# Graph attention on one core: rows of long neighbour lists searched whole, a slot index built in four parts, and a fourth slot for one row tile

## The chip, the cores and the metric

The kernel runs on one core of a Trainium2 chip. The metric is the device time of one launch in microseconds (us), taken as the median of several runs. Profiles come from one execution each; their times are us from the start of the span.

## The reference: what is computed

A pre-norm attention layer over a sparse graph. There are 16 batches of 1024 nodes with 512 features, and one adjacency matrix for all of them, in which a node has few neighbours (and always itself).

```python
h = relu(layernorm(x))                             # x: (16, 1024, 512)
q, k, v = h @ Wq + bq, h @ Wk + bk, h @ Wv + bv    # Wq, Wk, Wv: (512, 512); 8 heads of 64
scores = einsum('bihd,bjhd->bhij', q, k) / 8
scores = scores + where(adj == 0, -1e9, 0)         # adj: (1024, 1024), 0 or 1, diagonal 1
out = x + einsum('bhij,bjhd->bihd', softmax(scores), v)
```

## The kernel before

The kernel doesn't form the 1024 x 1024 scores. It sorts the nodes by degree and cuts them into eight tiles of 128 rows. Tile 0 holds the nodes with most neighbours, tile 7 those with fewest. Every row of tile t gets `CAPS[t]` slots, one neighbour each. Keys and values of a batch lie in DRAM as rows of 1024 numbers; a slot is one gather of 128 such rows. Tile 0 has rows with more neighbours than slots; what is left over is cut into pieces of four, which are worked on as one more tile, number -1.

The slots of a tile are worked on in units of two to four. A unit is (tile, first slot, slots); unit 0 is tile 7 and unit 2 is tile 5.

```python
CAPS = (11, 8, 6, 5, 4, 3, 3, 2)
PIECE = 4
PIECES = 17
LIST = CAPS[0] - 1 + PIECE * PIECES
ROUNDS = -(-LIST // 8)                             # 10
UNITS = (
    (7, 0, 2), (6, 0, 3), (5, 0, 3), (4, 0, 4), (3, 0, 3), (3, 3, 2), (2, 0, 3), (2, 3, 3),
    (1, 0, 4), (1, 4, 4), (0, 0, 4), (-1, 0, 4), (0, 4, 4), (0, 8, 3),
)
LAST_ORDER = (10, 11, 12, 13, 8, 9, 6, 7, 4, 5, 3, 2, 1, 0)   # the order of units in the last batch
POOL_FOLDS = (2, 3, 8, 9, 10, 11, 12)              # units whose folds of one slot are GpSimd's
BY_VECTOR = {2: 1, 3: 0, 4: 1}                     # slots of a unit that VectorE weighs; ScalarE the others
BY_VECTOR_LAST = {2: 1, 3: 1, 4: 2}                # the same in the last batch
```

What is done for a unit, with the line under which the profile lists it:

```python
def gather(i, s):         # L866, GpSimd's queue; a row's own node comes by SyncE's queue (L864)
    nc.gpsimd.indirect_dma_start(out=G[i][:, s]..., in_=KV[b % len(KV)][:], in_offset=on(ap=index[:, c + s : c + s + 1], axis=0))
def multiply(i):          # L876, DVE: keys times the tile's queries, which lie in PSUM
    nc.vector.tensor_tensor(k, k, Q[b, t][:, None, :].to_broadcast([P, count, D]), ALU.mult)
def score(i):             # L880, DVE: sums over each head
    nc.vector.tensor_reduce(weights[:, w, :], heads(G[i][:, :count, 0, :]), AX.X, ALU.add)
def exponent(i):          # L884, ACT
    nc.scalar.activation(weights[:, w, :], weights[:, w, :], AF.Exp, scale=HD**-0.5)
def weigh_v(i):           # L896, DVE: values of some slots times their weights
def weigh_s(i, s):        # L902, ACT: one slot, eight instructions
def fold(i, first, n):    # L907, DVE or GpSimd: adds n slots to n others
    engine = nc.gpsimd if n == 1 and i % NU in POOL_FOLDS else nc.vector
    engine.tensor_tensor(v[:, 0:n], v[:, 0:n], v[:, first : first + n], ALU.add)
# folds of a unit: {2: ((1, 1),), 3: ((2, 1), (1, 1)), 4: ((2, 2), (1, 1))}[count]
```

Per tile of rows and batch there are, besides: `load_x` (L590, GpSimd's queue), `stats` (L599, DVE), `variance` (L608, DVE), `power` (L611, GpSimd), `shift` (L615, DVE), `norm` (L625, ACT), `flip` (L632, PE transposes), `unflip` (L637, ACT), the projections to keys, values and queries (L642, PE), `evict_kv` (L653, ACT), `store_kv` (L665), `residual` (L966, GpSimd) and `put_out` (L969, GpSimd's queue). Keys and values of a batch are made while the batch before is attended to; PSUM holds the queries of two tiles.

The preparation, done once, ranks the nodes by degree, and tells each sorted row its node and the layernorm's numbers (table `told`), its own index and its first eight neighbours (table `lists`). Both tables are scattered through DRAM. For tile 0 all neighbours are needed, in falling order of a number that stands for the node:

```python
def spots():                                   # the slots of tiles 1 to 7
    merge("lists")
    for t in range(1, NT):
        c = first_col[t, 0]
        nc.vector.tensor_copy(spot[:, c : c + CAPS[t]], after["lists"][:, t, : CAPS[t]])
    slots(1)                                   # their index, in one piece
def long_rows():                               # L726: the 128 longest rows of adj, gathered
    ...
blocks, most = 16, 16
def long_blocks(k):
    row = LONG[0][:, 0, :]
    if k == 0:                                 # L734
        nc.vector.scalar_tensor_tensor(row, row, 0.0, key_row, op0=ALU.not_equal, op1=ALU.mult)
        return
    for c in range(4 * k - 4, 4 * k):          # L739 to L741: sixteen largest of each block of 64
        block = row.rearrange("p (k c) -> p c k", c=blocks)[:, c, :]
        got = LONG[0][:, 1, most * c : most * (c + 1)]
        nc.vector.max(got[:, 0:8], block)
        nc.vector.match_replace(block, got[:, 0:8], block, 0.0)
        nc.vector.max(got[:, 8:16], block)
def longest(k):                                # L747 to L751: rounds 1 to 9, eight numbers each
    row = LONG[0][:, 1, : most * blocks]       # 256 columns
    if k == 1:                                 # the first eight are known from the lists: take them out
        nc.vector.tensor_copy(found0[:, 0:8], after["lists"][:, 0, near])
        nc.vector.scalar_tensor_tensor(row, row, found0[:, 7:8], row, op0=ALU.is_lt, op1=ALU.mult)
    nc.vector.max(found0[:, ts(k, 8)], row)
    if k < ROUNDS - 1:
        nc.vector.match_replace(row, found0[:, ts(k, 8)], row, 0.0)
```

After the rounds, `count_pieces`, `owners`, `copy_owners` and `pieces` (DVE) with three small PE steps (L775, L785, L792) make the list of pieces, and `slots(0)` the index of tiles 0 and -1.

The order of the instructions on each engine isn't that of the text. A small list scheduler in the kernel sorts all steps by a place given to each, with rough lengths, and checks that a buffer is free; every engine then runs its instructions in that order.

## Time and profile before

| | |
|---|---|
| device time, median of three runs | 1755.13 us (1753.89 to 1758.23) |
| profiled span | 1752.1 us, 19712 instructions |
| mean granted TensorE clock | 0.97 |
| DMA | 531.73 MB, mean 303 GB/s |
| GpSimd gathers of slots (L866) | 608, 1030 ns each |
| ACT weighing (L902) | 4768 instructions, 340 ns each |

A line of the profile names the source line, the engine, the operation, the output and the inputs, the shape and the count. In the order of time, the first number is the start, the second the length, and square brackets at the end hold the idle time of the engine before the instruction and what ended it. GpSimd is called POOL, VectorE DVE, ScalarE ACT, TensorE PE. A busy time counts an instruction from start to end, also while it is held up inside.

### The profile page before, as it was taken

The page shows a single profiled execution, that of the slowest core. Times are in us where ns is not written, and L with a number is a line of the kernel's source. Part 1 is how long each engine was busy: PE and PEld are TensorE (multiplying, and loading weights), DVE is VectorE, ACT ScalarE, POOL GpSimd, SP SyncE. Part 2 cuts the span into 40 slices and gives each one's busy share as a digit, 9 for nine tenths or more (in the row PEclk, how much of TensorE's full clock was granted, in tenths as well). Part 3 has the DMA queues.
Part 4 walks back from the last instruction along what each step waited for, and adds up shares of the span by engine and source line. Part 5 has one row for each costly group of instructions (what it writes and reads, how often), then busy time and mean ns, then how long its engine had stood idle before and what let it go on. Part 6 is the DMA issues. An engine that isn't in the chain of part 4 may idle for free.

```text
span 1752.1 us, 19712 instructions
## 1 busy us (share of the span) xinstructions
PE 1618.9 (92%) x4295; PEld 751.8 (43%) x4295; DVE 1558.5 (89%) x1922; ACT 1489.1 (85%) x5556; POOL 1330.9 (76%) x1235
## 2 busy tenths in 40 slices
PE   6979898999999999999999999999999999999796
PEld 3444444444444444444444444444444444444333
DVE  5788989899898979989898998989989898988897
ACT  5359989898898988889898888989899898889965
POOL 4757778787787868877787877878787787877774
PEclk9989999999999999999999999999999999999989
DMA  5388889888898988988898888989988898888894
GB/s 219 132 321 293 309 292 344 309 324 316 287 329 304 339 298 309 323 284 327 305 350 303 304 304 293 346 318 328 322 294 313 293 346 304 318 311 290 310 359 169
DMA packets 150742, 531.73 MB, mean 303 GB/s; under 512 B 19916, under 2 KB 19916, under 8 KB 150616
## 3 DMA queue, kind: packets, MB, share of 16 engines
q0 software_dynamic: 109840, 390.70, 62.5%
q1 hardware_dynamic: 40776, 139.71, 21.7%
q8 instruction: 36, 0.59, 0.1%
q14 instruction: 90, 0.74, 0.1%
HBM read 429.51 MB, written 100.82 MB: 303 GB/s over the span
## 4 chain that ended last, share of the span: by engine, by line
PE 45%; DVE 18%; POOL 8%; ACT 6%; issue 4%; DMA 3%; POOLq 0%; DVEq 0%
PE pq L642 15%; PE pk L642 12%; PE pv L642 8%; DVE g L876 5%; ACT g L902 4%; PE acc L925 4%; DVE g L907 3%; DVE weights L880 3%; PE pht L632 3%; POOL g L866 3%; DVE shift L615 3%; DMA out_dram<-x,perm 2%; POOL x L966 2%; POOL g L907 1%; DVE g L896 1%
## 5 line engine op out<-in xcount | busy, mean ns | idle before, releaser
L902 ACT ACTIVATE g<-g,weights 128x64 f32<-128x64 f32 x4768 | 1180.3, 340 | 3.2 <-DVE weights L889 2.2
L866 POOL DMA_INDIRECT g<-kv,index x608 | 626.1, 1030 | 204.6 <-issue 143.5
L876 DVE TENSOR_TENSOR g<-g,pq 128x1536 f32<-128x1536 f32 (+2 forms) x208 | 389.1, 1872 | 95.4 <-PE pq L642 90.9
L642 PE MATMUL pq<-wq,hT 128*128 128x512 f32 x1024 | 460.3, 592 | 0.0
L642 PE MATMUL pk<-wk,hT 128*128 128x512 f32 x960 | 439.0, 601 | 1.8 <-ACT hT L637 1.7
L642 PE MATMUL pv<-wv,hT 128*128 128x512 f32 x960 | 431.6, 592 | 0.0
L880 DVE TENSOR_REDUCE weights<-g 128x32 f32<-128x2048 f32 (+2 forms) x224 | 423.2, 1890 | 0.6
L907 DVE TENSOR_TENSOR g<-g 128x512 f32<-128x512 f32 (+1 forms) x271 | 281.1, 1038 | 21.9 <-ACT g L902 19.8
L642 PEld LDWEIGHTS pq<-wq,hT 128*128 128x128 f32 x1024 | 194.7, 190 | 228.0 <-issue 224.7
L642 PEld LDWEIGHTS pk<-wk,hT 128*128 128x128 f32 x960 | 185.8, 194 | 212.9 <-issue 206.0
L642 PEld LDWEIGHTS pv<-wv,hT 128*128 128x128 f32 x960 | 182.5, 190 | 205.3 <-issue 201.9
L969 POOL DMA_INDIRECT out_dram<-x,perm x128 | 148.1, 1157 | 79.2 <-DMA out_dram<-x,perm 34.2
L625 ACT ACTIVATE h<-x,shift,rstd 128x512 f32<-128x512 f32 x120 | 91.3, 809 | 91.5 <-DVE shift L615 91.5
L590 POOL DMA_INDIRECT x<-in_x_dram,perm x128 | 135.9, 1062 | 34.9 <-issue 32.4
L907 POOL TENSOR_TENSOR g<-g 128x512 f32<-128x512 f32 x120 | 153.5, 1279 | 10.7 <-DVE g L907 7.2
L632 PE MATMUL pht<-ident,h 128*128 128x128 f32 x512 | 86.2, 308 | 80.2 <-ACT h L625 78.2
L632 PEld LDWEIGHTS pht<-ident,h 128*128 128x128 f32 x512 | 68.3, 158 | 139.5 <-ACT h L625 104.5
L896 DVE TENSOR_TENSOR g<-g,weights 128x512 f32<-128x512 f32 (+1 forms) x134 | 114.5, 855 | 2.2 <-ACT weights L884 1.7
L653 ACT COPY kvt<-pv 128x512 f32<-128x512 f32 x120 | 69.2, 577 | 43.0 <-PE pv L642 43.0
L966 POOL TENSOR_TENSOR x<-x,o 128x512 f32<-128x512 f32 x67 | 86.3, 1288 | 25.0 <-DVE o L957 22.1
L925 PE MATMUL acc<-g,ident 128*128 128x512 f32 x170 | 95.6, 682 | 2.8 <-POOL g L907 2.8
L637 ACT COPY hT<-pht 128x512 f32<-128x512 f32 x128 | 72.1, 575 | 26.9 <-PE pht L632 26.9
(231 smaller groups left out, 1187.0 us busy)
## 6 DMA issues: line engine op xcount, KB each, us to landing
g<-kv SPq DMA_DIRECT2D x128, 512.0 KB
kv<-kvt SPq DMA_DIRECT2D x120, 512.0 KB
g<-kv,index POOLq DMA_INDIRECT x608, 7.2
adj<-in_adj_dram SPq DMA_DIRECT2D x8, 512.0 KB
x_first<-in_x_dram SPq DMA_DIRECT2D x8, 256.0 KB
x<-in_x_dram,perm POOLq DMA_INDIRECT x128, 4.6
out_dram<-x,perm POOLq DMA_INDIRECT x128, 5.0
wk<-in_L_gnn_Wk_dram SPq DMA_DIRECT2D x1, 1024.0 KB
```

The lines of the kernel that those rows point to most:

```text
L590: nc.gpsimd.indirect_dma_start(out=X[n][:], out_offset=None, in_=x_rows, in_offset=on(ap=perm[:, t : t + 1], axis=0), element_offset=b * N * D
L632: nc.tensor.transpose(PH[n][:, c, :], hn[:, ts(c, P)], ident)
L642: nc.tensor.matmul(pt, HT[n][:, c, :], W[name][:, c, :], start=False, stop=(c == DC - 1))
L866: nc.gpsimd.indirect_dma_start(out=G[i][:, s].rearrange("p j d -> p (j d)"), out_offset=None, in_=KV[b % len(KV)][:], in_offset=on(ap=inde ...
L876: nc.vector.tensor_tensor(k, k, Q[b, t][:, None, :].to_broadcast([P, count, D]), ALU.mult)
L880: nc.vector.tensor_reduce(weights[:, w, :], heads(G[i][:, :count, 0, :]), AX.X, ALU.add)
L896: nc.vector.tensor_tensor(v, v, own.to_broadcast([P, n, H, HD]), ALU.mult)
L902: nc.scalar.activation(v[:, h, :], v[:, h, :], AF.Identity, scale=weights[:, c + s, h : h + 1])
L907: engine.tensor_tensor(v[:, 0:n], v[:, 0:n], v[:, first : first + n], ALU.add)
L925: nc.tensor.matmul(ACC[b, home], owner_t if t < 0 else ident, v[:, s, :], start=(u == parts_of(home)[0] and s == 0), stop=(u == parts_of(h ...
L966: (nc.vector if shares_in(b, B, t) and b == B - 1 else nc.gpsimd).tensor_tensor(rows, rows, add, ALU.add)
L969: nc.gpsimd.indirect_dma_start(out=out_rows, out_offset=on(ap=perm[:, t : t + 1], axis=0), in_=X.pop(b * NT + NT - 1 - t)[:], in_offset=No ...
```

## The change

Four things are different. Tile 5 has four slots in place of three, so unit 2 has four. The long rows are searched whole: the cut into blocks is gone, and each of the nine rounds reads the full row of 1024 columns; the first eight, which the lists hold already, are taken out beforehand as before. The slot index is made in four parts, each as soon as what it needs is there, so that gathers of the short tiles can start before the long rows are done. And the places in the plan are others: the `told` table is scattered before the `lists`, the x of batch 0 is loaded later, and most places of the repeated steps moved a little.

```diff
-CAPS = (11, 8, 6, 5, 4, 3, 3, 2)
+CAPS = (11, 8, 6, 5, 4, 4, 3, 2)
...
-    (5, 0, 3),
+    (5, 0, 4),
...
+PARTS = ((7, 6, 5), (4, 3), (2, 1), (0, -1))
...
-        add(("tell", t), "POOL", 1.3, -35.76 + 0.3 * t, ...
-        add(("spread", t), "POOL", 1.3, -28.64 + t, ...
+        add(("tell", t), "POOL", 1.3, -70.00 + 0.3 * t, ...
+        add(("spread", t), "POOL", 1.3, -30.76 + t, ...
...
-    for k in range(1, 5):
-        add(("long_blocks", k), "DVE", 2.0, -32.13 + 0.1 * k, [("long_blocks", k - 1)], [("g", -2)])
     for k in range(1, ROUNDS):
-        known = [("long_blocks", 4), ("spots",)] if k == 1 else [("longest", k - 1)]
-        add(("longest", k), "DVE", 1.1 if k == 1 else 0.8, --0.41 + 0.5 * k, known, [("g", -2)])
+        known = [("longest", 0), ("spots", 0)] if k == 1 else [("longest", k - 1)]
+        add(("longest", k), "DVE", 4.0 if k == 1 else 2.5, -3.25 + 0.5 * k, known, [("g", -2)])
...
-        p = (b - 1) * NU + j * rate if b > 0 else j * rate - 19.58 if b == 0 else 1.5 * j - 44.63
+        p = (b - 1) * NU + j * rate if b > 0 else j * rate - 8.00 if b == 0 else 1.5 * j - 44.25
...
-        stored = [("spots",) if t > 0 else ("slots", 0)] + [("store_kv", (b or -1) * NT + j) for j in range(NT)]
+        stored = [next(("spots" if t > 0 else "slots", k) for k, p in enumerate(PARTS) if t in p)] + [("store_kv", (b or -1) * NT + j) for j in range(NT)]
...
-        def spots():
-            merge("lists")
-            for t in range(1, NT):
+        def spots(k):
+            if k == 0:
+                merge("lists")
+            for t in PARTS[k]:
...
-            slots(1)
+            slots(k)
...
-        def longest(k):
-            row = LONG[0][:, 1, : most * blocks]
+        def longest(k):
+            row = LONG[0][:, 0, :]
+            if k == 0:
+                nc.vector.scalar_tensor_tensor(row, row, 0.0, key_row, op0=ALU.not_equal, op1=ALU.mult)
+                return
```

What the new places make of the order, as far as the prediction speaks of it (x8 and x9 are the first and second tile of the next batch; u2 is unit 2 of the batch at hand):

| engine | before | after |
|---|---|---|
| DVE, preparation | list_of 7, search in blocks, spots, longest 1 to 8, stats 8, longest 9, stats 9, count_pieces, variance 4, owners, shift 4, ..., multiply 0 | list_of 7, others, longest 0, spots 0, spots 1, longest 1, spots 2, longest 2, stats 8, ..., longest 6, shift 4, ..., longest 8, multiply 0, ..., longest 9, shift 5, ... count_pieces, multiply 4, ..., owners, ..., pieces, slots 3 |
| PE, preparation | ..., flip 5, 6, 7, three steps of the pieces, flip 8, 9, keys of 8 | ..., flip 8, 5, 9, 6, keys of 8, queries of tile 5, flip 10, ... |
| ACT, preparation | copy_row key, unflip of the third tile, rank_of 4 to 7 | copy_row key, norm, rank_of 4 to 7, unflip of the third tile |
| DVE, each batch | weigh_v u3, multiply u4, ..., multiply u5, fold u3, score u5, shift | weigh_v u2, ..., weigh_v u3, fold u2 (1024), multiply u4, ..., multiply u5, fold u3, shift, score u5 |
| PE, each batch | queries of tiles 7 and 6, add_up, queries of tile 5 | queries of tiles 7 and 6, keys of x8, add_up, queries of tile 5 |
| ACT, each batch | ..., weigh_s u2 0, evict x9, ... | ..., evict x9, weigh_s u2 0, weigh_s u2 1, evict x9, exponent u3, weigh_s u2 2 |
| POOL, each batch | fold u2, ..., fold u2, ..., power, fold u3, residual | put_out, fold u2, power, residual, ..., fold u3 |

## The prediction

> **What bounds the kernel now.** I read the page first, then the busy times in one window per batch, then the chain that ended last, then DVE, PE, ACT and POOL in order of time through one batch, then the preparation before 110 us.
>
> The page's first part shows four engines loaded, none full:
>
> ```profile
> PE 1618.9 (92%) x4295; PEld 751.8 (43%) x4295; DVE 1558.5 (89%) x1922; ACT 1489.1 (85%) x5556; POOL 1330.9 (76%) x1235
> ```
>
> The windows (window, length, then busy us and count of PE, PEld, DVE, ACT, POOL, granted clock, DMA share, GB/s):
>
> ```profile
> 98.00:202.00 104.00, 92.59 (x252) 44.43 (x253) 92.31 (x142) 84.24 (x308) 74.67 (x71) 0.93 0.87 312
> 409.00:512.00 103.00, 97.04 (x260) 45.11 (x259) 93.13 (x108) 91.92 (x350) 81.14 (x74) 0.98 0.88 315
> 1650.00:1752.00 102.00, 76.69 (x174) 32.77 (x174) 87.09 (x90) 68.07 (x280) 64.48 (x59) 0.88 0.70 263
> ```
>
> A batch repeats every 103.2 us (the first multiply of unit 4 stands at 445.36 in one batch and 548.58 in the next). PE has 97 us of work in it and DVE 93. A batch is longer than either, so a loop through several engines sets it. The chain of waits shows which: it runs on PE from 459 to 494, on DVE from 494 to 508, over ACT's layernorm to PE at 509, on PE to 434, and over DVE and POOL back to PE at 458. DVE in order of time (start, duration, line, shape, idle before and its releaser):
>
> ```profile
> 420.01 1.75 DVE L876 TENSOR_TENSOR g<-g,pq 128x1536 f32<-128x1536 f32 x1 [1.17 <-PE pq L642]
> 432.97 0.21 DVE L947 TENSOR_REDUCE sums<-weights 128x8 f32<-128x32 f32 x1 [1.25 <-ACT weights L884]
> 433.98 2.29 DVE L876 TENSOR_TENSOR g<-g,pq 128x2048 f32<-128x2048 f32 x1 [0.56 <-PE pq L642]
> 445.36 1.75 DVE L876 TENSOR_TENSOR g<-g,pq 128x1536 f32<-128x1536 f32 x1 [4.13 <-PE pq L642]
> 454.93 2.44 DVE L615 SCALAR_TENSOR_TENSOR shift<-mv,rstd 128x2 f32<-128x2 f32 x1 [0.54 <-POOL rstd L611]
> ```
>
> At units 0 to 3 DVE waits for PE's query projections, 4.13 us before unit 4. From unit 4 on it is the engine that makes PE wait. I therefore cut the batch at unit 4's multiply and at the end of the shift that releases the last layernorm, and asked for DVE's busy time in both parts:
>
> ```profile
> 445.36:507.95 62.59, 60.55 (x60) 1.00 0.88 319
> 507.95:548.50 40.55, 33.33 (x48) 0.96 0.89 319
> ```
>
> Full stretch: DVE busy 60.6 of 62.6. Slack stretch: 33.3 of 40.6, 7.2 idle, with PE full (39.65 busy of 40.55). The loop is DVE 62.6 plus PE 40.6. The 60.6 is not all work, as the next two pairs show:
>
> ```profile
> 456.10 1.25 POOL L966 TENSOR_TENSOR x<-x,g 128x512 f32<-128x512 f32 x1
> ...
> 464.45 1.27 POOL L966 TENSOR_TENSOR x<-x,g 128x512 f32<-128x512 f32 x1
> ```
>
> ```profile
> 463.88 2.40 DVE L907 TENSOR_TENSOR g<-g 128x512 f32<-128x512 f32 x1
> ```
>
> A shift of two columns is 0.15 us when alone (422.29) and was 2.44; a fold of 512 is 0.68 and was 2.40. Both end as POOL's additions end (457.35, 465.72). In this stretch such stretched records add 1.4, 2.3, 1.7, 0.5, 1.1 and 1.1, about 8 us.
>
> **What the Trainium skill says.** "SBUF — State Buffer", section "Who interferes with whom": a DVE instruction with two SBUF inputs contends with a GpSimd instruction that reads SBUF, and whoever comes second blocks for the whole instruction. The trace agrees with the two pairs above; multiplies, whose second input is in PSUM, keep 2.29 us beside POOL folds (493.95). "VectorE: DVE Perf Modes", section "The perf-mode tier table (the rule you actually need)": fp32 tensor_tensor and tensor_reduce run at one element per cycle, 2293 ns for 2048. The trace has 2.28 and 2.27, so a slot costs its elements and nothing hides in a faster mode. "Perfetto Trace Analysis", section "Optimization Strategy", says to look for gaps within a regime, since the most contended engine may change over time; that is the cut above.
>
> **The change, part by part.**
>
> *The fourth slot of tile 5 (unit 2), each batch.* DVE: multiply and score go from 1536 to 2048 elements (1.75 to 2.28 and 1.73 to 2.27, +1.07). Units of four give one slot to DVE's weighing (+0.69) and one fold of 1024 to DVE (+1.21): +3.0 us. ACT still weighs three slots. POOL loses one of two folds (-1.28) and issues one more gather (0.95 + 0.30): nothing. DMA moves 0.52 MB more per batch of some 32 MB, +1.6%. PE is unchanged. All 3.0 us lie between the last shift and unit 4's multiply, in the stretch with 7.2 us idle. By the built order, the DVE work from unit 4's multiply to that shift is the same set of instructions in both kernels, and so is PE's set from there to unit 4's queries. So I expect the slot not to lengthen the loop.
>
> Does it fit? In the new order the queries of unit 2 come one projection later (428.1 in the old clock instead of 424.5), those of unit 3 and 4 stay at 434 and 445.2. DVE from 434: multiply 2.2, two folds and the small ones 1.8, score 2.2, weighings 1.2, fold 1.15, so about 443. But ACT evicts the keys of the next batch's second tile, from PE at 438.1, ahead of unit 2's weighings: 0.5 + three weighings at 1.93 + one eviction 0.5 + an exponent 0.2 ends at 445.1, the fold at 446.4. Unit 4 starts about 1 us late.
>
> *The full stretch.* POOL's second fold of unit 2, beside which a DVE fold of 1024 took 2.58 instead of 1.22 (450.68), is gone: -1.3. The layernorm's power stands earlier in POOL's order, ahead of a residual and folds, and the shift on DVE right behind unit 3's fold. So the flip that made PE wait 2.0 us at 458.27 comes in time, and DVE starts unit 6 at about 456.3, as its queries arrive, not at 458.19: -1.9, part of it the same time as the -1.3. Against +1 for the fold, the loop loses about 1 us. The other stretched records may fall better or worse. I take -1.0 per batch with an uncertainty of 1.3, over the 14 to 15 batches from the first unit 4 on: -14 us, give or take 19.
>
> *The preparation.* DVE's search of the long rows, in order of time before:
>
> ```profile
> 73.84 1.22 DVE L734 SCALAR_TENSOR_TENSOR adj_long<-adj_long,rows 128x1024 f32<-128x1024 f32 x1 [5.39 <-DMA adj_long<-in_adj_dram,perm]
> 75.10 0.27 DVE L739 MAX8 adj_long<-adj_long 128x8 f32<-128x64 f32 x1
> ...
> 92.62 0.48 DVE L748 SCALAR_TENSOR_TENSOR adj_long<-adj_long,found 128x256 f32<-128x256 f32 x1
> ...
> 104.97 0.15 DVE L615 SCALAR_TENSOR_TENSOR shift<-mv,rstd 128x2 f32<-128x2 f32 x1
> ```
>
> The blocks go: 75.1 to 88.5, -13.4 us. The rounds now read 1024 columns instead of 256. A MAX8 of 1024 has 1228 ns (list_of's row) against 424, a MATCH_REPLACE8 I estimate at 408 + 800. So a round is about 2.6 instead of 0.98 us, eight rounds +12.8, the masking and the last maximum +1.5. The search costs as much as before. The index in four parts adds two pairs of small instructions, +0.7.
>
> What moves is order. The first part of the index needs only the lists, and stands at about 77 instead of 92. But the first multiply follows eight rounds on DVE, and comes at about 106, as before (106.87). What gains is PE. The shift for batch 1's first layernorm, before the last thing to end (104.97), now follows six rounds. PE stood idle before it:
>
> ```profile
> 103.37 0.59 PE L775 MATMUL p_before<-has,owner_t 128*128 128x1 f32 x2 [7.77 <-DVE owner_t L772]
> ```
>
> Counting DVE on from lists at 75, with 2.6 a round and 0.9 a statistic, that shift ends at 99.5. From its flip to unit 4's queries PE has 28.6 us of work, one wait of about 1, so these end at 130 instead of 134.9: -5. Against it: the longest-row pieces and part of the slots (some 4 us of DVE) now fall into batch 0's full stretch, which had 5 us idle; ACT ranks tiles before it copies the third flipped tile, so PE stores batch 0's keys some 6 us later, and the lists start 3 us later, which the tables scattered first only partly win back. Net -2, between -6 and +4. Loading batch 0's x later costs nothing, its first use is behind those stores.
>
> *The tail.* Unit 2 stands in the last four of the last batch, where DVE and PE alternate without slack: +1.07 +0.6 on DVE: +1.7.
>
> Sum: 1755.1 - 14 - 2 + 1.7 = 1741; a little caution gives 1742.
>
> **Rivals.** First, DVE is the bound and every microsecond of the slot counts: 15 x 3.0 + 1.7, no gain at the loop: about 1800. For it: DVE at 93 of 103 and continuous from 463 to 512. Against it: the 7.2 us idle exactly where the slot falls. Second, the ACT order in front of unit 2's weighings takes the slack: +1 to +2 per batch without the gains behind it, about 1770 to 1780. For it: 92 of 103 busy, DVE waits 1.25 us for it at 432.97 already. Third, PE becomes the bound at 97.6 us per batch, its waits all gone: 15 x -5.6, about 1672. Against it: the 4 us wait at 508.85 behind DVE remains. Fourth, only preparation counts and the loop stays: 1755.
>
> **Range and chances.** The loop's uncertainty of 19 and the preparation's 4 give 1716 to 1774. Faster by over 2% (below 1720) needs -2.3 us per batch: 0.15. Slower by over 2% (above 1790) is the first rival: 0.05. Within: 0.80.
>
> **What would show it.** Right: unit 4's multiply repeating every 101 to 103 us, DVE's idle at units 0 to 3 down to 4 or less, the flip at 458 without a wait, PE's hole before 104 gone and batch 0's unit 4 at 129 to 132. Wrong: the period above 104, DVE or PE waiting for ACT's weighing of unit 2, or more stretched folds and shifts than about 8 us a batch.

## The result: half a per cent slower, and where the time lies

The changed kernel takes 1764.97 us (median of 4 runs, 1762.67 to 1765.71), the kernel before 1754.51 (1753.84 to 1758.23): ratio 1.0053, 95% interval 1.0036 to 1.0070. I had forecast 12.5 us less; it is 10.5 us more. The range held it, the sign was wrong. Two further comparisons of the same two kernels gave 1.0059 (1.0039 to 1.0078) and 1.0058 (1.0045 to 1.0071).

"Batch n" below runs from unit 4's multiply of batch n to that of the next. Two pairs of traces (that of the first comparison, whose chips are not on record, and e5 and e6 of the experiments, both from one chip) place the loss:

| us | before | after | before, second pair | after, second pair |
|---|---|---|---|---|
| unit 4 of batch 0 starts | 134.9 | 136.4 | 135.3 | 137.4 |
| batch 0 | 102.8 | 103.9 | 102.8 | 103.9 |
| batch 3 | 103.2 | 111.9 | 104.3 | 109.5 |
| batch 12 | 103.6 | 107.1 | 102.7 | 107.0 |
| the other eleven of batches 1 to 13, mean | 103.97 | 103.67 | 103.53 | 103.50 |
| from unit 4 of batch 14 to the end | 164.0 | 164.3 | 165.2 | 164.4 |
| span | 1752.1 | 1763.9 | 1749.0 | 1760.7 |

The eleven ordinary batches gained 3.3 us in all in one pair and 0.3 in the other. Batches 3 and 12 lost 12.2 and 9.6, the preparation with batch 0 2.6 and 3.2.

### The profile page after: what moved, and what is told of

The parts are those of the page before. It is cut to its first block, busy times and chain, and to the rows that moved or that the text cites. A ratio compares the mean times of both kernels' runs of the same rounds, so it can differ in the third digit from the quotient of the medians.

```text
span 1763.9 us, 19726 instructions
## 1 busy us (share of the span) xinstructions
PE 1629.2 (92%) x4297; PEld 752.7 (43%) x4297; DVE 1574.6 (89%) x1892; ACT 1495.9 (85%) x5556; POOL 1305.7 (74%) x1236
## 4 chain that ended last, share of the span: by engine, by line
PE 34%; DVE 15%; DMA 11%; POOL 10%; issue 8%; ACT 8%; POOLq 0%; DVEq 0%; ACTq 0%
PE pq L642 12%; PE pk L642 8%; DMA g<-kv,index 7%; ACT g L890 6%; PE pv L642 6%; DVE g L895 5%; PE acc L913 4%; POOL g L854 4%; DVE weights L868 4%; DVE g L864 3%; DMA out_dram<-x,perm 3%; POOL x L954 3%; PE pht L632 2%; DMA x<-in_x_dram,perm 2%; POOL out_dram L957 1%
## 5 line engine op out<-in xcount | busy, mean ns | idle before, releaser
L854 POOL DMA_INDIRECT g<-kv,index x624 | 643.3, 1031 | 202.1 <-issue 141.5
L868 DVE TENSOR_REDUCE weights<-g 128x32 f32<-128x2048 f32 (+2 forms) x224 | 432.5, 1931 | 0.6
L864 DVE TENSOR_TENSOR g<-g,pq 128x2048 f32<-128x2048 f32 (+2 forms) x208 | 396.4, 1911 | 33.4 <-PE pq L642 15.7
L895 DVE TENSOR_TENSOR g<-g 128x512 f32<-128x512 f32 (+1 forms) x286 | 305.4, 1068 | 20.0 <-ACT g L890 19.6
L957 POOL DMA_INDIRECT out_dram<-x,perm x128 | 133.1, 1040 | 86.0 <-DMA out_dram<-x,perm 29.9
L590 POOL DMA_INDIRECT x<-in_x_dram,perm x128 | 129.6, 1013 | 46.8 <-issue 34.4
L632 PE MATMUL pht<-ident,h 128*128 128x128 f32 x512 | 89.9, 310 | 79.2 <-ACT h L625 75.3
L895 POOL TENSOR_TENSOR g<-g 128x512 f32<-128x512 f32 x105 | 134.7, 1283 | 18.4 <-DVE g L895 16.7
L653 ACT COPY kvt<-pk 128x512 f32<-128x512 f32 x120 | 69.1, 576 | 47.4 <-PE pk L642 46.9
```

Of the source, the lines that this page charges most:

```text
L590: nc.gpsimd.indirect_dma_start(out=X[n][:], out_offset=None, in_=x_rows, in_offset=on(ap=perm[:, t : t + 1], axis=0), element_offset=b * N * D
L632: nc.tensor.transpose(PH[n][:, c, :], hn[:, ts(c, P)], ident)
L854: nc.gpsimd.indirect_dma_start(out=G[i][:, s].rearrange("p j d -> p (j d)"), out_offset=None, in_=KV[b % len(KV)][:], in_offset=on(ap=inde ...
L957: nc.gpsimd.indirect_dma_start(out=out_rows, out_offset=on(ap=perm[:, t : t + 1], axis=0), in_=X.pop(b * NT + NT - 1 - t)[:], in_offset=No ...
```

## The profile after

The first part of the page of the changed kernel, busy times of the five engines:

```profile
PE 1629.2 (92%) x4297; PEld 752.7 (43%) x4297; DVE 1574.6 (89%) x1892; ACT 1495.9 (85%) x5556; POOL 1305.7 (74%) x1236
```

DVE is up 16.1 us, where the slots alone are 45 (15 x 3.0); shorter stretched records (1.3 us a batch, below) make up some 20 of the difference. POOL is down 25.2.

The windows of the changed kernel (window, length, then busy us and count of PE, PEld, DVE, ACT, POOL, granted clock, DMA share, GB/s): batch 9, cut where the prediction cut its batch, and batch 3.

```profile
1077.61:1138.90 61.29, 57.24 (x151) 25.59 (x149) 59.53 (x61) 57.27 (x217) 47.13 (x45) 1.00 0.87 317
1138.90:1181.93 43.03, 42.08 (x110) 20.17 (x111) 36.08 (x50) 35.98 (x137) 31.67 (x30) 0.92 0.89 318
445.44:557.29 111.85, 102.80 (x263) 47.69 (x262) 92.55 (x110) 94.47 (x358) 84.39 (x77) 0.94 0.84 301
```

The same two stretches of batch 9 in the kernel before:

```profile
1070.19:1132.04 61.85, 57.52 (x153) 26.06 (x151) 59.82 (x60) 56.94 (x215) 51.45 (x46) 1.00 0.89 318
1132.04:1172.95 40.91, 40.01 (x108) 19.33 (x109) 33.34 (x50) 35.82 (x137) 29.94 (x28) 0.96 0.88 315
```

In this batch the full stretch is 0.6 shorter and the slack stretch 2.1 longer. In the slack stretch DVE has 2.7 us more work, the slot, and still 7 us idle: the slot fits, as forecast. But PE is busy 2.1 us longer, with two more records, at a granted clock of 0.92 instead of 0.96.

What DVE waited for between 300 and 1600 us (releaser, us in all, times, longest), before:

```profile
DVE g L876 <- PE pq L642: 80.4, 45, 4.1
DVE sums L947 <- ACT weights L884: 16.2, 13, 1.2
DVE shift L615 <- POOL rstd L611: 4.8, 9, 0.5
DVE st L599 <- DMA x<-in_x_dram,perm: 0.3, 1, 0.3
```

and after:

```profile
DVE sums L935 <- ACT weights L872: 29.2, 13, 2.4
DVE st L599 <- DMA x<-in_x_dram,perm: 23.2, 13, 2.7
DVE o L945 <- PE acc L913: 14.2, 11, 2.3
DVE g L864 <- PE pq L642: 12.5, 13, 3.1
DVE shift L615 <- POOL rstd L611: 12.0, 7, 4.2
DVE g L864 <- DMA g<-kv,index: 7.7, 10, 3.0
```

The idle at the queries of units 0 to 4 is mostly filled. Five waits are new or grown: the row sum in front of unit 4 waits 2.2 us a batch for an exponent, the statistic behind unit 4's multiply waits 1.8 for a load of x, the output of a tile waits for PE's sums, the shift for GpSimd's power, and multiplies wait for gathers. DVE around unit 4 after, in order of time:

```profile
1178.88 0.22 DVE L935 TENSOR_REDUCE sums<-weights 128x8 f32<-128x40 f32 x1 [2.41 <-ACT weights L872]
...
1180.79 1.23 DVE L895 TENSOR_TENSOR g<-g 128x1024 f32<-128x1024 f32 x1 [0.50 <-ACT g L890]
1181.93 1.75 DVE L864 TENSOR_TENSOR g<-g,pq 128x1536 f32<-128x1536 f32 x1
```

Unit 4's queries were done at 1180.94 (here and below: when PE starts its next record), so the multiply is 1.0 late; before, it followed its queries by 0.2 in every batch. ACT in the same time shows why:

```profile
1173.84 0.59 ACT L653 COPY kvt<-pk 128x512 f32<-128x512 f32 x1 [2.94 <-PE pk L642]
1174.33 3.93 ACT L890 ACTIVATE g<-g,weights 128x64 f32<-128x64 f32 x16
1178.16 0.56 ACT L653 COPY kvt<-pv 128x512 f32<-128x512 f32 x1
1178.63 0.23 ACT L872 ACTIVATE weights<-weights 128x32 f32<-128x32 f32 x1
```

ACT stands 2.94 us before the keys of the next batch's second tile, and the weighings and the exponent come behind them.

PE at its second wait of batch 9, before:

```profile
1132.94 1.97 PE L632 MATMUL pht<-ident,h 128*128 128x128 f32 x8 [3.96 <-ACT h L625]
1134.70 1.77 PE L925 MATMUL acc<-g,ident 128*128 128x512 f32 x2
...
1136.67 3.60 PE L642 MATMUL pk<-wk,hT 128*128 128x512 f32 x8
```

and after:

```profile
1139.85 1.12 PE L632 MATMUL pht<-ident,h 128*128 128x128 f32 x4 [4.81 <-ACT h L625]
1140.76 1.92 PE L913 MATMUL acc<-g,ident 128*128 128x512 f32 x2
1142.47 1.06 PE L632 MATMUL pht<-ident,h 128*128 128x128 f32 x4
...
1143.99 4.47 PE L642 MATMUL pq<-wq,hT 128*128 128x512 f32 x8
```

Behind the wait PE is slow in both kernels: eight transposes take 1.97 or 2.18 us (1.04 at 96.77 us in e6), two sums 1.77 or 1.92 (1.02 at 1151.91 before), and in this batch after also the first projection, 4.47 for 3.60. That last differs from batch to batch: of batches 4 to 11 two have such a slow projection before (4.54 and 4.55) and two after (4.44 and 4.47). The next 32.6 us of PE are the same to 0.01 in both kernels (1140.10 to 1172.75, and 1148.30 to 1180.94). "TensorE: Matmul & The Clock Gate", section "HAM oscillation — how this bites in real kernels", says that an idle gap of PE of more than about 3.4 us throttles it, so that the work behind the gap starts at half clock. The trace agrees: behind waits of 3.96 and 4.81 the transposes and sums take nearly twice as long, and the granted clock is below 1 in this stretch and 1.00 in the other.

Over batches 4 to 11 the means are, by stretches:

| us | before | after | before, second pair | after, second pair |
|---|---|---|---|---|
| unit 4 to the end of PE's second wait | 63.56 | 62.49 | 62.98 | 62.35 |
| DVE in it: stretched records, excess | 8.18 | 6.75 | 7.96 | 6.73 |
| DVE in it: waits | 1.68 | 2.52 | 1.40 | 2.45 |
| PE's first wait in it | 1.69 | 0.53 | 1.49 | 0.75 |
| from there to the end of the first projection (slow start) | 7.49 | 7.57 | 7.59 | 7.61 |
| from there to the end of unit 4's queries | 32.64 | 32.64 | 32.64 | 32.64 |
| unit 4's multiply late by | 0.20 | 1.27 | 0.20 | 1.05 |
| batch | 103.89 | 103.97 | 103.41 | 103.65 |

(Excess is the sum over records of what they took above the tenth percentile of their shape, where that is over 0.3 us.)

Last, GpSimd in batch 3:

```profile
444.13 1.01 POOL L957 DMA_INDIRECT out_dram<-x,perm  x1 [4.63 <-DMA out_dram<-x,perm]
447.18 2.00 POOL L590 DMA_INDIRECT x<-in_x_dram,perm  x1 [2.04 <-issue]
...
459.37 0.73 POOL L611 TENSOR_TENSOR rstd<-rstd,minus_half 128x2 f32<-128x2 f32 x1
```

and DVE behind it:

```profile
460.13 0.16 DVE L615 SCALAR_TENSOR_TENSOR shift<-mv,rstd 128x2 f32<-128x2 f32 x1 [4.19 <-POOL rstd L611]
```

A store of the output waits for the transfer of the store before it, the load behind it waits 2.04 us for nothing that the profile names (called a hole from here on) and takes 2.00 instead of 1. The power comes late, and with it the shift, the layernorm and PE; how much of that is the hole's, the experiments tell. In batch 12 the same hole stands before a load of x, and the shift waits 2.17:

```profile
1456.09 1.01 POOL L590 DMA_INDIRECT x<-in_x_dram,perm  x1 [2.02 <-issue]
```

## The experiments

All kernels keep the planned order of the kernel that they start from; the edits move entries in the finished list (`ahead(key, of)` and `behind(key, of)`), so that nothing else shifts. Their lines lie some places lower than in the listings. Ratios are to the kernel before on the same chip.

**The slot alone, and without it.**

```diff
 # on the kernel before: the fourth slot of tile 5, the old order
-    (5, 0, 3),
+    (5, 0, 4),
+    order.insert(at(("gather", k, 2)) + 1, ("gather", k, 3))      # k: unit 2 of each batch
+    order.insert(at(("weigh_v", k + 1)), ("weigh_v", k))          # and a fold of two slots for that of one
```

> The kernel before with the fourth slot of tile 5 alone, all other steps in their old order (one more gather behind the third, weigh_v ahead of unit 3's, the fold of 1024 on DVE ahead of unit 4's multiply). Theory: the 3.0 us of DVE fit into the idle time at units 0 to 3, and the loss of the change lies in its order and its preparation: 1755 to 1762 us (1.7 for the tail, at most 0.3 a batch), and DVE's wait for the queries of unit 4 falls from 4.1 to about 1 us. Rival, DVE is the bound and the slot counts in full: 15 x 3.0 + 1.7, about 1800. Rival, the slot costs as much as the whole change: about 1765.

```diff
 # on the changed kernel: three slots again, everything else as it is
-    (5, 0, 4),
+    (5, 0, 3),
+    order.remove(("gather", k, 3)); order.remove(("weigh_v", k))
```

> The changed kernel with three slots for tile 5 (one gather, one weigh_v and DVE's fold of 1024 fewer; the fold goes to POOL), all other steps in the changed order. Theory: the order is what costs, the slot little: 1757 to 1765. Rival, DVE is the bound: 1765 - 47, about 1718. Rival, the slot costs what the change lost: about 1755.

**Two waits of the changed kernel, one by one.**

```diff
 # the load of x that the statistic behind unit 4 needs
+    ahead(("load_x", 8 * b + 13), ("residual", b, 6))
```

> The changed kernel with one step moved in each batch from the third on: the load of the next batch's sixth x tile goes ahead of the residual of tile 6 and of a gather on POOL's queue, as in the kernel before. Theory: the wait of DVE's statistic for this x, 2.7 us behind unit 4's multiply in 12 or so batches, is what ate the 2 us by which the full stretch should have become shorter; without it a batch is 1.5 to 2.5 us shorter: 1735 to 1750. Rival, the wait hides another one that ends as late (the flip behind POOL's power): 1760 to 1765.

```diff
 # ACT copies the third flipped tile before it ranks
+ahead(("unflip", -6), ("rank_of", 4))
```

> The changed kernel with one step moved in the preparation: ACT copies the third flipped tile (unflip -6) ahead of the four ranks and not behind them, as in the kernel before. Theory: PE's key projection no longer stands 4.6 us in front of the rank row, the lists start 4 us earlier, and the first unit 4 is at 132 instead of 136.4: 1760 to 1762. Rival, the preparation is held by POOL's scatters or by DVE's rounds: first unit 4 at 135 to 136, 1764 to 1765.

Measured, on a chip where the kernel before takes 1808.9 us instead of 1755: 1.0030 (1.0012 to 1.0047), 0.9838 (0.9795 to 0.9881), 0.9855 (0.9821 to 0.9889), 0.9851 (0.9815 to 0.9886). The slot in the old order costs 0.3%, 5.2 us, where the first rival says 45: it is refuted. In e1 unit 4 follows its queries by 0.26 us, with all the work of the slot in front of it. e2, e3 and e4 lie within 0.2% of each other, and the changed kernel itself was not run there, so what the slot, the load or the flip is worth in the new order can't be read from them. But the whole family of the changed order is 1.5% faster than before on this chip, against 0.5% slower in the first comparison. In their preparation engines stand still for reasons that the profile doesn't name. PE in e4:

```profile
113.77 1.11 PE L644 MATMUL pht<-ident,h 128*128 128x128 f32 x4 [9.17 <-issue]
```

Unit 4 of batch 0 comes at 146.6 (e1, e2) to 154.9 (e3), 10 to 18 us later than in the first pair. A batch of e1 is 107.4, one of e2 to e4 104.5 to 105.2. So this chip answers little about a change of 0.5%, and the next edits ran beside both kernels themselves.

**The kernels again, and both waits taken away.**

> The kernel before, unchanged, for a trace on the same chip as the others of this call. On the chip of the first experiments it took 1809 us against 1755 in the first comparison, and the time from unit 4's multiply to the pieces' multiply (full stretch) of the slot-added kernel was 52.6 us there against 48.6 in the first trace of before. Theory (this order leans on transfers that land just in time, and a chip whose transfers are slower lengthens its full stretch): the period is above 106 us on a chip where it takes over 1790 us, with the excess in the full stretch and in waits for DMA there; on a chip where it takes 1755 us the period is 103.9 and full stretch 48.6. Rival (the chip only lengthens the preparation): period 103.9 +-0.5 on either chip and unit 4 of batch 0 later than 150 us. Ratio 1.000 either way.

> The changed kernel, unchanged. Theory (the change itself is worth nothing in the loop, and the sign depends on where a chip puts the preparation and the transfers): about 1785 us and ratio 0.985 to 0.99 if the chip is the one of the first experiments, 1765 us and 1.005 if it is one like that of the first comparison; period 104.5 either way. Rival (the four-slot unit costs a fixed amount everywhere): ratio 1.005 on any chip, that is 1818 us where before takes 1809.

```diff
 # on the changed kernel (7): the load as above, and unit 3's exponent ahead of unit 2's weighings
+    ahead(("load_x", 8 * b + 13), ("residual", b, 6))
+    ahead(("exponent", 14 * b + 3), ("weigh_s", 14 * b + 2, 0))
```

> The changed kernel with two places in the order moved: GpSimd issues the sixth x load of a batch ahead of the residual of the third tile, and ScalarE does unit 3's exponent ahead of unit 2's weighings. If my two waits (statistic on x 24.6 us over 14 batches, row sum on exponent 29.2 us over 13) are what ate the expected gain in the full stretch, the period falls from 104.5 to 102.5 to 103.5 and the time by 10 to 28 us against the unchanged changed kernel. Rival (the waits only show where the slack of the loop lies, PE and DVE being behind anyway): the waits go, others take their place, period 104.0 to 104.8, time within 6 us of the unchanged changed kernel.

```diff
 # (8): these two, the third flipped tile first, and three slots again
+    ahead(("unflip", -6), ("rank_of", 4)); order.remove(("gather", k, 3)); order.remove(("weigh_v", k))
```

> The changed kernel with three slots for tile 5 again (every sixth neighbour of it goes to the pieces as before), the two moves of the run above, and ScalarE copying the third flipped tile ahead of the ranks in the preparation. If the slot lies in idle time of DVE, it ends within 5 us of the same kernel with the slot; if it still takes part in setting unit 4's start (1.2 us a batch in the slack stretch), it is 12 to 20 us faster than the unchanged changed kernel and the fastest of this call. Keys of batch 0 stored some 5 us earlier than in the changed kernel, unit 4 of batch 0 at 3 to 5 us earlier.

Before takes 1756.8 here: 1.0000 (0.9988 to 1.0012), 1.0059 (1.0039 to 1.0078), 1.0089 (1.0067 to 1.0111), 1.0022 (1.0010 to 1.0034). e5 and e6 are the second pair of the tables: batches 3 and 12 repeat to 2.3 and 0.1 us. In e7 both waits go, and unit 4 to PE's second wait falls to 61.19, 1.2 less than in e6. The time does not: the lateness of unit 4 rises from 1.05 to 2.64, and batches 4 to 11 average 103.84 against 103.65. The time is as the rival had it, but for the load this shows little, since the second edit makes unit 4 late by itself: with unit 3's exponent ahead, ACT waits 1.48 us for DVE's scores of unit 3 at the end of batch 5, unit 2's weighings come behind, and DVE's fold waits 4.58 for the third. The load alone was not run where before takes 1755 us. PE's waits for normalized rows between 660 and 1280 us, in e5, e6 and e7 (us, times, longest):

```profile
PE pht L632 <- ACT h L625: 33.6, 12, 4.0
```

```profile
PE pht L632 <- ACT h L625: 33.0, 10, 4.8
```

```profile
PE pht L654 <- ACT h L647: 33.1, 12, 4.8
```

Six batches, 5.5 to 5.6 us each, in all three: what one wait of PE loses, the other gains here. In e8, without the slot, unit 4 follows its queries by 0.20 again, batch 3 takes 103.1 and batch 12 102.9, and the mean of batches 4 to 11 is 104.0. So without the slot the two long batches are gone, and the ordinary batches are no faster: e8 saves 5.3 us against e6, less than the 9.6 that these two batches had lost. The earlier flip in the preparation moved unit 4 of batch 0 by 0.5 us (136.9 against 137.4).

**Batches 3 and 12, and the shift of the preparation.**

```diff
 # (9) batch 3's GpSimd order as in the later batches
+behind(("load_x", 37), ("gather", 49, 0)); behind(("fold", 44, 1, 1), ("put_out", 3, 6))
+behind(("residual", 3, 5), ("power", 18)); behind(("load_x", 39), ("residual", 3, 5))
 # (10) two tiles of x loaded a second time while GpSimd waits in batch 0
+order[at(("gather", 5, 1)) + 1 : at(("gather", 5, 1)) + 1] = [("again", 12), ("again", 13)]
 # (11) the shift of batch 1's first layernorm earlier on DVE
+behind(("stats", 9), ("longest", 4)); behind(("variance", 4), ("stats", 9))
+behind(("power", 4), ("variance", 4)); behind(("shift", 4), ("longest", 5))
 # (12) all three
```

> The changed kernel with batch 3's GpSimd order made like that of the later batches (the sixth x load behind the third residual and the next gather, two more swaps). In the changed kernel the period from batch 3's unit 4 to batch 4's is 111.9 and 109.5 us in two traces, against 103.7 for its other batches, and batch 12's is 107.1 and 107.0. Theory A (batch 3's own order makes it long, through the x load that stands early there): batch 3's period falls to 103 to 105, batch 12's stays at 107, the time falls 4 to 7 us. Theory B (a hole of 2.0 us in GpSimd's issue, which stands before the 220th indirect transfer of the program whatever it is, makes batch 3 and, at the 750th, batch 12 long): batch 3 stays above 108, because the 220th transfer is still in the same place.

> The changed kernel with two more indirect transfers on GpSimd in the preparation: two x tiles are loaded a second time, in a stretch where GpSimd waits. All later indirect transfers of GpSimd count two more, and nothing else moves. Theory B (the hole comes at the 220th and 750th transfer by count): both holes of 2.0 us stand two transfers earlier, batch 3 and batch 12 lose 2 us or more of their excess of 6 to 8 and 3.5 us, or keep it with the hole at another instruction; the hole is not before the x load any more. Theory A (batch 3's order): the period of batch 3 stays 109 to 112, and the hole stays before the x load at the same instruction. The first unit 4 is not more than 2 us later.

> The changed kernel with the statistic, variance, power and shift that release batch 1's first layernorm put one to two rounds of the search earlier on VectorE. My prediction rested on TensorE running without waits from that shift to unit 4's queries (28.6 us); measured are 33.5, with TensorE waiting 1.79 and 1.43 us and one key projection of eight taking 5.51 instead of 3.60. Theory (that shift still sets when unit 4 of batch 0 starts): shift at 98 instead of 101.6, unit 4 of batch 0 2 to 4 us earlier (133 to 135 instead of 136.4 to 137.4), time 2 to 4 us lower. Rival (the start of batch 0 is set by the rounds on VectorE and the first multiply at 107.7, TensorE only follows): unit 4 of batch 0 within 1 us of 137, time unchanged within 2 us.

> The three edits of this call together. If each is worth what its theory says (batch 3 and 12: 6 to 11 us, the preparation 2 to 4), the changed kernel comes out 8 to 14 us faster than unchanged, 1751 to 1757 where before takes 1756, that is no slower than before: the loss against before would then be these places and not the slot. If it stays within 4 us of the unchanged changed kernel, the loss is spread over all batches.

Before takes 1755.0: 1.0074 (1.0047 to 1.0101), 1.0023 (1.0006 to 1.0039), 1.0044 (1.0031 to 1.0057), 1.0047 (1.0028 to 1.0066). Counted through the program, the hole of batch 12 stands before GpSimd's 750th indirect transfer, that of batch 3 before the 220th. In e10 the 750th is another instruction, a store:

```profile
1442.58 1.01 POOL L976 DMA_INDIRECT out_dram<-x,perm  x1 [2.05 <-issue]
```

The hole goes with the count, and batch 12 takes 102.8 instead of 107: the hole stands 11.5 us earlier in the batch, and the shift that had waited 2.17 us for GpSimd waits 1.24. In e9, where the 220th is a gather, the hole is there too:

```profile
453.27 0.96 POOL L870 DMA_INDIRECT g<-kv,index  x1 [1.74 <-issue]
```

and batch 3 takes 107.6; in e10, where the 220th is a gather among gathers, no hole stands before it and batch 3 takes 106.3. So for batch 12 theory B holds: where before takes 1755 us, that batch is 105.3 to 107.7 in the six traces with the hole before that load, and 102.7 to 104.8 in the three with two transfers more. Batch 3 is part hole only. In e10 its shift waits as long as in the changed kernel:

```profile
461.29 0.16 DVE L634 SCALAR_TENSOR_TENSOR shift<-mv,rstd 128x2 f32<-128x2 f32 x1 [4.20 <-POOL rstd L630]
```

The power that it waits for stands on GpSimd behind two residuals, three gathers, a load, an addition and a store, so this wait comes from batch 3's own order. In e9, which changes that order, the wait is gone, but DVE waits 3.06 us for a gather, and with both edits (e12) 4.63, and batch 3 takes 110.0. Why the two gains don't add stays open. e10 is the best of the four-slot kernels run where before takes 1755 us. Against the ratios of the unchanged kernel on other chips it makes more than half of the loss good; on this chip that kernel wasn't run, and e12, which contains e10's edit, missed its 1751 to 1757 with 1763.1 us.

e11: the shift ends 3.4 us earlier than in e6 (starts at 99.33 and 102.71), and unit 4 of batch 0 starts at 137.2 (e6 137.4). PE in e11:

```profile
105.28 3.60 PE L657 MATMUL pk<-wk,hT 128*128 128x512 f32 x8
112.07 0.38 PE L655 MATMUL pq<-bq_parts,chosen 128*128 128x512 bf16 x1 [3.19 <-DVE g L879]
```

PE does its key projection 3.5 us earlier than in e6 and then waits 3.19 for DVE's first multiply, which frees the buffer of the queries: PSUM holds those of two tiles. The time is as the rival had it, but the edit moved more than the shift. The first multiply comes at 110.80, in e6 at 108.79:

```profile
110.80 1.22 DVE L879 TENSOR_TENSOR g<-g,pq 128x1024 f32<-128x1024 f32 x1 [2.22 <-issue]
```

GpSimd waits 2.29 us for the earlier power's input there, and issues the first gather of a slot at 101.82, in e6 at 99.35. So e11 shows that PE can't run ahead of that multiply, and not that the earlier shift is worth nothing.

**Unit 4 in time, alone and with the rest.**

```diff
 # (13) on the changed kernel, batches 1 to 14: n = 8 * b + 9, k = 14 * b + 2
+    behind(("evict_kv", n, 0), ("weigh_s", k, 2)); behind(("evict_kv", n, 1), ("evict_kv", n, 0))
+    behind(("store_kv", n), ("evict_kv", n, 1))
 # (14) with the two extra transfers; (15) and with the load of x ahead
```

> The changed kernel with one move on ScalarE in batches 1 to 14: the keys (and values) of the next batch's second tile are evicted behind unit 2's third weighing instead of ahead of the first. In the traces of the changed kernel unit 4's multiply starts 1.0 us after its queries are there (0.20 in the kernel before), behind a fold that waits for ScalarE's third weighing and a row sum that waits 2.4 us for an exponent. Theory (the eviction, for which ScalarE waits 2.94 us on TensorE, is what makes unit 4 late, and the slot's work only exposes it): lateness of unit 4 down from 1.0 to 0.2, period 0.5 to 0.9 us shorter, time 7 to 12 us below the unchanged changed kernel, ratio to before 0.999 to 1.002. Rival 1 (the slot's own VectorE work makes it late): lateness stays 0.8 to 1.0 and the ratio 1.004 to 1.006. Rival 2 (TensorE then waits for the buffers of keys): lateness falls, a new TensorE wait takes its place, ratio 1.004 or more.

> The move of the run above and the two extra indirect transfers of the preparation that took batch 12 from 107 to 102.8 us and batch 3 from 109.5 to 106.3. If the two causes add: 3 to 6 us below the run above, ratio to before 0.996 to 1.000, so that the four-slot kernel is no slower than before. If they don't add: within 2 us of the run above.

> The run above and the sixth x load of each batch issued ahead of the third residual. The statistic's wait of about 1.7 us a batch on that load goes. If the stretch from unit 4 to the second wait of TensorE is still part of the loop, the period falls by another 0.3 to 1.0 us and the ratio to 0.988 to 0.996, faster than the kernel before; if TensorE then only waits longer and starts slower, within 3 us of the run above.

On a chip where before takes 1792.5: 0.9994 (0.9975 to 1.0014), 0.9953 (0.9930 to 0.9975), 0.9878 (0.9844 to 0.9913). In e13 the lateness falls to 0.20 or less in 9 of the batches 1 to 14. DVE at unit 4 of batch 6:

```profile
775.25 1.22 DVE L914 TENSOR_TENSOR g<-g 128x1024 f32<-128x1024 f32 x1 [0.26 <-ACT g L909]
776.68 1.75 DVE L883 TENSOR_TENSOR g<-g,pq 128x1536 f32<-128x1536 f32 x1 [0.21 <-PE pq L661]
```

The multiply now waits for its queries (done at 776.48) with the slot's work in place. So it takes both to make unit 4 late, the slot and ACT's order: it is not late in the old order with the slot (e1, 0.26 us), nor in the new order without it (e2 and e8, 0.20), nor, in most batches, with both once that eviction is moved. The ratio hit what was expected of e13, but on such a chip that proves nothing, since the unchanged kernel was not beside it. In e16 to e18 it is.

> The changed kernel, unchanged, beside the next two on one chip. On two chips where before takes 1755 us it took 1.0053 and 1.0059 of that. Theory (the change trades a fixed loss in a few places for less dependence on transfers that land late): 1.004 to 1.007 where before takes 1755 us, 0.984 to 0.998 where before takes 1790 us or more. Rival (the ratio is a property of the kernels alone): 1.004 to 1.007 on any chip.

```diff
 # (17) is (15) again
```

> The three moves on the changed kernel together (keys of the next batch's second tile evicted behind unit 2's weighings, sixth x load ahead of the third residual, two extra indirect transfers), beside the unchanged one. In the last call it took 0.9878 of before on a chip where before took 1792 us, with a period of 104.0. Theory (the moves are worth 6 to 10 us on any chip): 0.990 to 0.996 of the changed kernel on this same chip. Rival (the moves only help where transfers are late): within 0.3% of the changed kernel where before takes 1755 us.

> The kernel before, for its trace beside the other two. If before takes 1790 us or more here: theory (its loop leans on transfers just in time) period 106 to 108 with the excess over 103.5 in the stretch from unit 4 to TensorE's second wait; rival (only the preparation is longer) period 103.5 to 104.2 and unit 4 of batch 0 at 148 us or later. If before takes 1755 us, period 103.5 to 103.9 as in the two traces so far.

Before takes 1757.2: 1.0058 (1.0045 to 1.0071), 1.0041 (1.0018 to 1.0064), 0.9997 (0.9982 to 1.0011). e17 takes 1767.7, the unchanged kernel 1768.1. The three moves are worth nothing on this chip. Batch 12 is 104.8 and batch 3 106.5, against 106.6 and 109.1 in e16 (whose trace is of its slowest run, 1774.4); but batches 4 to 11 average 104.1 against 104.3, and unit 4 is late again, by 1.15 us, with the eviction moved. (On the chip of e14 and e15, which differ only in that load of x, it was late by 0.36 without it and 0.93 with it.) With the load ahead, GpSimd's residual falls beside the slot's work on DVE; at the end of batch 7 a fold that takes 1.22 alone takes 2.75:

```profile
970.55 2.75 DVE L927 TENSOR_TENSOR g<-g 128x1024 f32<-128x1024 f32 x1 [0.49 <-ACT g L922]
```

No version was found that beats the kernel before where that takes 1755.

## Why the prediction was wrong, step by step

**That the slot fits: right.** The rival that counts all of its 3.0 us was refuted by e1 (5 us, not 45), and in the changed kernel DVE has 7 us idle in the slack stretch with the slot in it.

**Unit 4 about 1 us late: right, in size and in the main in cause.** Measured +1.07 and +0.85 us; e13 moved the eviction that I had named and most of the lateness went. In e17 it came back beside GpSimd's residual.

**The full stretch, -2: this is the step of the loop that failed.** It gave -1.07 and -0.63. Its first half was right: the records stretched beside GpSimd's additions fell by 1.43 and 1.23 us where I had 1.3, in line with "SBUF — State Buffer", section "Who interferes with whom", that the prediction used. (Of its two pairs the shift ends with the addition, at 457.37 and 457.35, but the fold 0.56 us behind it.) (Of its two pairs the shift ends with the addition, at 457.37 and 457.35, but the fold 0.56 us behind it.) The second half, -1.9 "as the flip comes in time", did not come. I had DVE start unit 6 as its queries arrive. It starts 1.67 and 1.85 us behind the last record of these queries, where before it was 1.60 and 1.40 (batches 4 to 11). PE's first wait did shrink, by 1.16 and 0.74, but DVE's waits grew by 0.84 and 1.05: the statistic behind unit 4's multiply waits 1.65 and 1.88 us a batch for the load of x that now stands on GpSimd behind a residual and a gather (0.03 and 0.00 before). That load ahead again takes this wait away, but in e17 unit 6 is still 1.45 behind; what takes its place stays open. And of what PE gained it handed 0.71 and 0.54 to its second wait (3.92 to 4.63, 3.96 to 4.50), as DVE's last shift came no earlier than that. Counted from the end of unit 4's queries, the stretch is 63.76 us in both kernels of the first pair, 63.18 and 63.40 in the second: it is shorter only because it starts later, at a late unit 4. I had looked for waits that go, and not, in the new order of GpSimd, for what its queue holds back.

From PE's second wait to unit 4's queries there is next to nothing, +0.07 and +0.02 us. So the sum for an ordinary batch is -1.07 + 0.07 + 1.07 = +0.1, and -0.63 + 0.02 + 0.85 = +0.2, where I had -1.0. Against -1.0 a batch, the eleven ordinary batches fell short by 7.7 and 10.7 us in all, batches 3 and 12 by 14.2 and 11.6, and batch 0 by 2.2 in either pair.

**"A batch repeats": wrong for two of fourteen.** I read one batch and multiplied. Batch 3 is the last before the order becomes periodic, and holes in GpSimd's issue come at fixed counts of transfers. Before, the hole at the 750th transfer stood in front of a gather at 1467.9 us; with the slot's further gathers (16 in the program) it stands in front of a load of x for which GpSimd has no slack. Without the slot, in the new order, it is a gather again (e2 and e8). The two batches are most of the loss, 12.2 and 9.6 us. e10 shows the hole as the cause for batch 12; batch 3, which lost 8.6 and 5.3 us, is 5.6 and 3.2 shorter without it, and the shift's wait there comes from GpSimd's order.

**The preparation, -2: wrong sign.** Shift at 101.57 where I had 99.5, unit 4 of batch 0 at 136.4 where I had 130.

```profile
101.57 0.15 DVE L615 SCALAR_TENSOR_TENSOR shift<-mv,rstd 128x2 f32<-128x2 f32 x1
...
107.70 1.22 DVE L864 TENSOR_TENSOR g<-g,pq 128x1024 f32<-128x1024 f32 x1 [0.21 <-PE pht L632]
```

```profile
102.67 1.36 PE L632 MATMUL pht<-ident,h 128*128 128x128 f32 x8 [1.79 <-ACT h L625]
105.46 1.97 PE L632 MATMUL pht<-ident,h 128*128 128x128 f32 x8 [1.43 <-ACT hT L637]
...
107.65 5.51 PE L642 MATMUL pk<-wk,hT 128*128 128x512 f32 x8
113.00 0.38 PE L640 MATMUL pq<-bq_parts,chosen 128*128 128x512 bf16 x1
```

The search itself costs what I had (1.23 and 1.21 us for the two instructions of a round; 1.23 and 1.21 expected), and the first multiply is at 107.7 where I had 106. The step that failed is "from its flip to unit 4's queries PE has 28.6 us of work, one wait of about 1". In the changed kernel PE waits 1.79 and 1.43 in it, and its key projection takes 5.51 where one takes 3.60 later on. With the shift's end 2.2 us behind my count, the 2.2 us more of waiting and the 1.9 of the slow projection come to 6.3 of the 6.4 us by which unit 4 missed 130. After that projection PE goes on to the queries at 113.00 without a wait, the first multiply being over at 108.9: here it did not wait for it, other than in e11. Why the shift came later than counted stays open. Batch 0's own +1.1 was not taken apart; the pieces and slots that now fall into it, which I had named, are a likely cause, not shown.

**The tail, +1.7:** measured +0.3 and -0.8. **The range:** its terms, -14 give or take 19, -6 to +4 and +1.7, add up to 1718 to 1766, not to 1716 to 1774.

**Open.** Where before takes 1790 to 1810 us, kernels with the changed order take 0.984 to 0.999 of it; the changed kernel itself was not run there. e1, the old order with the slot, has batches of 107.4 there, and DVE waits longer in its loop; no trace of the kernel before itself was taken on such a chip; e18, meant for it, ran where that kernel takes 1757. So why those chips favour the new order wasn't settled.

## What to carry to other kernels

A wait that goes is a gain only if the engine that waited is on the path there; in a loop that two engines close together, PE's other wait took back 0.7 of the 1.2 us that one of its waits lost, and the loop got no shorter. Before multiplying one batch by their number, measure all of them: two of fourteen held most of this loss. And after moving work off a queue, read what the queue now holds in front of a transfer that somebody needs.

## What was not expected of the hardware

GpSimd's issue of indirect transfers has holes that go with the count: 1.69 to 2.05 us before the 750th in 18 of 20 traces, three slots or four (1.70 before, 2.02 after, 2.05 in e10), and 0.54 in e15 and e17. The counts have a step: from the 100th transfer on, the 20 traces have 54 holes of between 1.6 and 2.3 us (idle time of GpSimd before an indirect transfer to which the profile names no releaser), and 52 of them stand before the 114th, 220th, 326th, 432nd, 750th or 856th, all a multiple of 106 apart. No trace has one at every such count, and the kernel before, with its 220th a load of x too, has 0.30 us there. So the count says where a hole can stand, not that it does. "DMA: Bandwidth & Descriptors", section "SWDGE vs HWDGE vs iDMA", says that GpSimd writes the descriptors of its transfers into rings; a wrap of such a ring would count like this, but that is a guess, and no run here shows the cause.

The same program, the kernel before, takes 1754.5 to 1757.2 us in four comparisons and 1792.5 and 1808.9 in two, on two other chips; that is up to 3%, six times the effect under study. Kernels with the changed order were up to 1.6% faster than it on those two, where the unchanged one was not run, so the sign of the effect may turn with the chip. A ratio from one chip is shown for chips like it.
